# A graph-network layer: node stages in quads with transposes ahead, alphas and sums a step behind, target rows as three bf16 parts

## The chip, the cores and the metric

The kernel runs on one core of a Trainium2 chip. Its time is device microseconds, the median of several runs. Lines (L718) are those of the kernel before.

## What is computed

12,500 nodes with 128 channels, 400,000 edges sorted by target. All is fp32. In short:

```
h        = relu(layernorm(x))
message  = (h @ w_src + b_src)[src] + (h @ w_dst)[dst]
message *= edge_weight * (silu(silu(edge_attr @ w1 + b1) @ w2 + b2) @ w3 + b3)
sep      = message @ w_sep + b_sep           # per head (8): 16 for alpha, 16 for value
score    = sum_k smooth_leaky_relu(alpha)[k] * alpha_dot[k]
att      = softmax of score over the edges of one target
out      = x + segment_sum(value * att, dst) @ w_proj + b_proj
```

## The kernel before

**Node stage** (L140 to L290). x lies in SBUF as 98 tiles of 128 nodes, in groups of 14. For each group `stats` (layer-norm statistics on VectorE) and `norm` (ScalarE) of the next group are issued, then `products` of this one: for each quad of four tiles transposes on TensorE (L220), a VectorE copy `hT` (L223), products with both weight matrices (L230), and two copies out of PSUM, `ms`, one on ScalarE (L237) and one on VectorE that adds b_src (L238). The two tables of messages, `t_src` and `t_dst`, go to DRAM. After group 1, `ends_and_cuts` checks on VectorE that the edges are sorted and narrow enough for the fast path, and writes the first and last target of every section to DRAM.

**Setup of the windows** (L603 to L634): small loads of the doubled MLP weights, the windows' first targets (`tgt`) and `far`, all on SP's queue.

**The window loop** (`passes`, from L636; `step(k)`, k from -5 to 399). A step is 1000 edges in two sections of 500, each of four tiles of 125. A section's targets lie in a window of 64 nodes. The order of instructions on each engine is the order in which `step` issues them by hand:

- SP: the stores of step c-1, loads of edge weights, targets (`load_d`), the two windows' rows of `t_dst` (`load_md`), edge attributes (`load_e`, one of a step's eight tiles for eight steps at once) for later steps. c = k - 12 (`LAG`).
- `gather(k+4)`: eight indirect DMAs by GpSimd (L718) fetch the source rows into `gs`, of which there are four; each block waits for the last transposes of step k.
- `sums_begin(c)`: softmax weights copied into `pvx` (ScalarE), one-hot rows of targets `oh` (VectorE, L851).
- `mlp3(k)` (L758, then `rad` on VectorE, L761) and `message(k)`: eight transposes of gathered rows into PSUM (L770), onto which the target rows are accumulated as an fp32 one-hot product of 64 rows, one for each section (L775); `mT` = that times `rad` (L779).
- `values(c, 0)`, `alphas(k, 0)`, `values(c, 1)`: V = mT @ w_v of the step twelve back (L864), times weights into `pvx` (L866); pa = w_a @ mT (L783), its silu `sl` (L785) and `al` (L787).
- `mlp1(k+2)`, `mlp2(k+1)` (h on ScalarE, L739 and L746), `one_hot_T(k+1)` (`ohT`), `alphas(k, 1)`.
- `sums(c)`: 16 small products of `oh` and `pvx` (L875), copied out as `ob` (L879), stored in the next step.
- parts of the softmax of earlier steps, `e_T(k+3)` (transposes of edge attributes, L728), and in odd steps `scores(k)` of two steps (L794).

PSUM has eight banks: p3 two (shared by mlp1 and mlp3), m1 (mlp2 and e_T), pm two, pa, V, and `misc` (sums, scores, softmax and index transposes).

After the loop the last twelve steps are drained, partial sums of nodes that cross sections are combined and scattered into `agg` (L1067). **Final stage** (from L1130): groups of 14 tiles; GpSimd adds b_proj to x (L1162), VectorE divides by the weights' sums (L1165 to L1168), quads are transposed (L1179), copied (L1182), multiplied by w_proj (L1186), and x and a bias of the values are added on VectorE (L1185, L1190). A slower path for unsuitable inputs exists and isn't taken.

Of the kernel before, what the change touches and what calls it, by code (L numbers as in the profile page):

```python
# [21 lines left out]
F32 = mybir.dt.float32  # L22
# [30 lines left out]
LAG = 12  # L53
EP = 8
# [3 lines left out]
def gnn_kernel(ctx: ExitStack, tc: tile.TileContext, a: dict, out: bass.AP):  # L58
# [18 lines left out]
    agg = dram.tile([N + W, ROW], F32, name="agg")  # L77
    win = dram.tile([NS * W, ROW], F32, name="win")
    base_d = dram.tile([2, NP], I32, name="base_d")
# [15 lines left out]
    x_v = x[0:NF * P, :].rearrange("(p t) c -> p t c", t=NF)  # L95
    ident = const.tile([P, P], F32, name="ident")
# [48 lines left out]
    with tc.tile_pool(name="node", bufs=2) as np_, tc.tile_pool(name="node1", bufs=1) as n1, \  # L145
# [6 lines left out]
        b_nodes = n1.tile([P, C], F32, name="b_nodes")  # L152
        nc.scalar.dma_start(out=b_nodes, in_=a["b_src"].to_broadcast([P, C]))
# [6 lines left out]
        last = n1.tile([1, 2, NP], I32, name="last")  # L160
# [3 lines left out]
        nc.sync.dma_start(out=prev[1:RP, :], in_=dst[RC - 1:E - 1].rearrange("(p c) -> p c", c=RC))  # L164
        with nc.allow_non_contiguous_dma(reason="the sections' ends"):
            for f in range(2):
                nc.sync.dma_start(out=base[:, f, :], in_=dst_h[f:f + 1, :, 0])
                nc.sync.dma_start(out=last[:, f, :], in_=dst_h[f:f + 1, :, SEC - 1])
# [16 lines left out]
        spans = groups[:-1] + [(groups[-1][0], NB)]  # L185
        hs = {}

        def rows(t):
            return P if t < NF else tail

        def stats(g):
            t0, t1 = spans[g]
            for t in range(t0, t1):
                n = rows(t)
                st = np_.tile([P, nc.vector.BN_STATS_DIM], F32, name="st", bufs=4)
                nc.vector.bn_stats(st[:n], x_all[:n, t, :])
                nc.vector.bn_aggr(mv[:n, t, :], st[:n])
            s = slice(t0, t1)
            nc.scalar.activation(rstd[:, s], mv[:, s, 1], AF.Sqrt, bias=eps, scale=1.0)
            nc.vector.reciprocal(rstd[:, s], rstd[:, s])  # L200
            nc.vector.scalar_tensor_tensor(shift[:, s], mv[:, s, 0], -1.0, rstd[:, s],
                                           op0=ALU.mult, op1=ALU.mult)

        def norm(g):
            t0, t1 = spans[g]
            hs[g] = np_.tile([P, XG, C], F32, name="h")
            for t in range(t0, t1):
                n = rows(t)
                nc.scalar.activation(hs[g][:n, t - t0, :], x_all[:n, t, :], AF.Relu,
                                     bias=shift[:n, t:t + 1], scale=rstd[:n, t:t + 1])  # L210

        def products(g):
            t0, t1 = spans[g]
            ms = np_.tile([P, 2, XG, C], F32, name="ms")
            for u0 in range(t0, t1, 4):
                us = range(u0, min(u0 + 4, t1))
                pt = nps.tile([P, 4, P], F32, name="pt")
                for u in us:
                    n = rows(u)
                    nc.tensor.transpose(pt[:, u - u0, :n], hs[g][:n, u - t0, :], ident[:n, :n])  # L220
                hT = np_.tile([P, 4, P], F32, name="hT")
                w = (len(us) - 1) * P + rows(us[-1])
                nc.vector.tensor_copy(hT.rearrange("p u n -> p (u n)")[:, :w],  # L223
                                      pt.rearrange("p u n -> p (u n)")[:, :w])
                for v0 in range(0, len(us), 2):
                    vs = us[v0:v0 + 2]
                    pm = nps.tile([P, 2, 2, C], F32, name="pm", bufs=4)
                    for j, u in enumerate(vs):
                        n = rows(u)
                        nc.tensor.matmul(pm[:n, j], hT[:, u - u0, :n], w_nodes, start=True, stop=True)  # L230
                    i, m = vs[0] - t0, len(vs)
                    if rows(vs[-1]) == P:
                        cuts = [(P, 0, m)]
                    else:
                        cuts = [(P, 0, m - 1)] * (m > 1) + [(tail, m - 1, m)]
                    for n, j0, j1 in cuts:
                        nc.scalar.copy(ms[:n, 0, i + j0:i + j1, :], pm[:n, j0:j1, 0, :])  # L237
                        nc.vector.tensor_tensor(  # L238
                            ms[:n, 1, i + j0:i + j1, :], pm[:n, j0:j1, 1, :],
                            b_nodes[:n].unsqueeze(1).to_broadcast([n, j1 - j0, C]), op=ALU.add)  # L240
            f1 = min(t1, NF)
            for k, table in enumerate((t_src, t_dst)):
                tv = table[0:NF * P, :].rearrange("(p t) c -> p t c", t=NF)
                nc.sync.dma_start(out=tv[:, t0:f1, :], in_=ms[:, k, 0:f1 - t0, :])
# [4 lines left out]
        def ends_and_cuts():  # L249
# [5 lines left out]
            ends = n1.tile([1, 2 * NS + 2], I32, name="ends")  # L255
            nc.vector.memset(ends, -1)
            ev = ends[:, 1:2 * NS + 1].rearrange("o (k f c) -> o f k c", f=2, c=2)
            nc.vector.tensor_copy(ev[:, :, :, 0], base)
            nc.vector.tensor_copy(ev[:, :, :, 1], last)
            nc.sync.dma_start(out=base_d.rearrange("f k -> (f k)").unsqueeze(0),  # L260
                              in_=base.rearrange("o f k -> o (f k)"))
            nc.sync.dma_start(out=ends_d, in_=ends)
            nc.sync.dma_start(out=t_dst[N:N + W, :], in_=z[:W, 0:C])
            span = n1.tile([1, 2 * NP], F32, name="span")
            nc.vector.tensor_sub(span, last.rearrange("o f k -> o (f k)"),
                                 base.rearrange("o f k -> o (f k)"))
            nc.vector.tensor_scalar(span, span, float(W - 1), None, op0=ALU.is_ge)
            wide = n1.tile([1, 1], F32, name="wide")
            nc.vector.tensor_reduce(wide, span, AX.X, ALU.add)
            gt = n1.tile([RP, RC], BF16, name="gt")  # L270
            nc.vector.tensor_tensor(gt, prev, cur, op=ALU.is_gt)
            cnt = n1.tile([RP, 1], F32, name="cnt")
            nc.vector.tensor_reduce(cnt, gt, AX.X, ALU.add)
            tot = nps.tile([1, 1], F32, name="tot", bufs=1)
            nc.tensor.matmul(tot, cnt, ones[:RP, 0:1], start=True, stop=True)
            nc.vector.tensor_add(bad, tot, wide)

        G = len(spans)
        stats(0)
        norm(0)  # L280
        for g in range(G):
            if g + 1 < G:
                stats(g + 1)
                norm(g + 1)
            products(g)
            if g == 1:
                ends_and_cuts()
        w_score = const.tile([C, C], F32, name="w_score")
        nc.vector.tensor_scalar(w_score, heads, dot, 0.8, op0=ALU.mult, op1=ALU.mult)
# [313 lines left out]
    def windows():  # L603
        with tc.tile_pool(name="wk", bufs=1) as kp:
            w1b = kp.tile([P, P], F32, name="w1b")
            nc.vector.memset(w1b, 0.0)
            w2b = kp.tile([P, P], F32, name="w2b")
            nc.vector.memset(w2b, 0.0)
            w3b = kp.tile([P, C], F32, name="w3b")
            b12 = kp.tile([P, 2], F32, name="b12")  # L610
            for f in range(2):
                for q in range(2):
                    r = (2 * q + f) * RAD
                    nc.sync.dma_start(out=w1b[r:r + RAD, f * FC:(f + 1) * FC], in_=a["fc_w1"])
                s = slice(f * FC, (f + 1) * FC)
                nc.sync.dma_start(out=w2b[s, s], in_=a["fc_w2"])
                nc.sync.dma_start(out=w3b[s, :], in_=a["fc_w3"])
                nc.sync.dma_start(out=b12[s, 0:1], in_=a["fc_b1"])
                nc.sync.dma_start(out=b12[s, 1:2], in_=a["fc_b2"])
            w_s = kp.tile([C, 32], F32, name="w_s")  # L620
            nc.vector.memset(w_s, 0.0)
            nc.vector.tensor_copy(w_s[:, 0:H], w_score[:, 0:C:C // H])
            b_s = kp.tile([P, 1], F32, name="b_s")
            tgt = kp.tile([P, NP], F32, name="tgt")
            far = kp.tile([P, NS], BF16, name="far")
            with tc.tile_pool(name="tg", bufs=1) as gp, tc.tile_pool(name="tg_ps", bufs=1, space=PSUM) as gq:
                pb = gq.tile([P, 1], F32, name="pb")
                for j in range(4):
                    nc.tensor.matmul(pb[32 * j:32 * j + 32, :], w_s, b_a, start=True, stop=True)
                nc.vector.tensor_scalar(b_s, pb, 0.25, None, op0=ALU.mult)  # L630
                tb = gp.tile([P, NP], I32, name="tb")
                nc.sync.dma_start(out=tb[0:W, :], in_=base_d[0:1, :].to_broadcast([W, NP]))
# [605 lines left out]
```

## Time and profile before

| what | value |
|---|---|
| median of three runs | 6562.58 us (6560.19 to 6575.51) |
| profiled execution | 6566.2 us, its span 6564.2 us |
| granted TensorE clock, mean | 0.873 |
| busy PE / DVE / ACT / POOL | 77% / 44% / 27% / 47% |
| node stage | 0 to 194 us |
| setup, up to the first mlp3 | 194 to 239 us |
| 400 steps, first mlp3 to last | 239 to 6296 us |
| drain and combine | 6296 to 6410 us |
| final stage | 6410 to 6564 us |

PE is TensorE's matmuls, PEld its weight loads, DVE VectorE, ACT ScalarE, POOL GpSimd, SP the queue that issues most DMAs. A group's row gives line, engine, operation, output and input, count, then busy time, mean ns of one, and the engine's idle time just before it with what ended it. A timeline row gives start, duration, the instruction, and in brackets the idle time before it. An end of a matmul in the trace is modelled, so the time at which others get its result is seen in their starts.

### The profile page before, as it was taken

How to read it: one execution, taken by the hardware profiler on the slowest of the kernel's cores; microseconds unless marked ns; L12 is line 12 of the kernel's file. 1: busy time of each engine (PE TensorE's matmuls, PEld its weight loads, DVE VectorE, ACT ScalarE, POOL GpSimd, SP SyncE). 2: the span in 40 equal slices, each digit the busy share in tenths (PEclk: the TensorE clock that was granted, in tenths of full speed). 3: DMA queues.
4: the chain of work that ended last, by engine and by line, in shares of the span. 5: the costliest groups of instructions: out<-in, count | busy, mean ns of one | idle time of the engine just before them, and what ended most of it. 6: DMA issues, size and time to landing. Idle time of an engine off the chain costs nothing. (4 is left out here: it accounts for less than half of the span.)

```text
span 6564.2 us, 79188 instructions
## 1 busy us (share of the span) xinstructions
PE 5066.2 (77%) x26490; PEld 2665.6 (41%) x26490; DVE 2887.1 (44%) x5210; ACT 1785.1 (27%) x3797; POOL 3111.5 (47%) x3231
## 2 busy tenths in 40 slices
PE   3477878787878878788788787887887878888774
PEld 2234444444444444444444444444444444444453
DVE  4234444444444444444444444444444444444465
ACT  3122222222222222222222222222222222222221
POOL 0455555455554545544455454454554545545402
PEclk7688898898998989988888898898888989888885
DMA  3454444444444444444444444444444444444423
GB/s 124 135 144 119 124 119 115 125 117 121 121 122 118 121 119 119 124 117 115 123 120 121 119 116 121 122 115 120 121 117 122 119 120 121 124 119 118 114 60 123
DMA packets 884920, 783.25 MB, mean 119 GB/s; under 512 B 527255, under 2 KB 773279, under 8 KB 884250
## 3 DMA queue, kind: packets, MB, share of 16 engines
q1 hardware_dynamic: 778482, 560.72, 31.0%
q0 software_dynamic: 102816, 210.37, 13.6%
q10 hardware_dynamic: 3202, 6.99, 0.3%
q8 instruction: 212, 3.47, 0.2%
q14 instruction: 208, 1.70, 0.1%
HBM read 643.82 MB, written 134.27 MB: 119 GB/s over the span
## 5 line engine op out<-in xcount | busy, mean ns | idle before, releaser
L718 POOL DMA_INDIRECT gs<-t_src,idx x3200 | 3067.4, 959 | 3189.3 <-PE pm L770 1756.2
L787 DVE SCALAR_TENSOR_TENSOR al<-pa,sl 128x500 f32<-128x500 f32 x800 | 542.9, 679 | 1570.9 <-ACT sl L785 1022.1
L761 DVE SCALAR_TENSOR_TENSOR rad<-p,c_fc_b,w_b 128x500 f32<-128x500 f32 x800 | 553.6, 734 | 1389.4 <-PE p L758 1102.0
L783 PE MATMUL pa<-mT,c_w_a 128*128 128x500 f32 x1600 | 833.7, 603 | 256.8 <-DVE mT L779 248.1
L785 ACT ACTIVATE sl<-pa,c_b_a 128x500 f32<-128x500 f32 x800 | 541.4, 677 | 1789.4 <-PE pa L783 626.9
L864 PEld LDWEIGHTS V<-c_w_v,mT 128*125 128x125 f32 x6208 | 741.2, 188 | 634.8 <-issue 337.9
L864 PE MATMUL V<-c_w_v,mT 128*125 128x128 f32 x6208 | 891.3, 286 | 23.2 <-issue 1.1
L794 PE MATMUL misc<-al,w_s 128*32 128x500 f32 x1600 | 365.9, 986 | 539.5 <-ACT ob L879 525.3
L779 DVE TENSOR_TENSOR mT<-pm,rad 128x500 f32<-128x500 f32 x800 | 504.3, 672 | 280.1 <-PE pm L775 252.8
L758 PE MATMUL p<-h,w3b 64*128 64x500 f32 x1600 | 625.5, 870 | 0.0
L770 PEld LDWEIGHTS pm<-ident,gs 125*128 125x128 f32 x3200 | 430.1, 169 | 435.9 <-issue 435.9
L866 DVE TENSOR_TENSOR pvx<-V,Pem 125x512 f32<-125x512 f32 x776 | 528.9, 682 | 44.4 <-PE m L744 26.5
L770 PE MATMUL pm<-ident,gs 125*128 125x125 f32 x3200 | 533.6, 321 | 0.0
L875 PEld LDWEIGHTS misc<-pvx,oh 125*64 125x64 f32 x6400 | 365.5, 137 | 322.4 <-issue 279.7
L875 PE MATMUL misc<-pvx,oh 125*64 125x136 f32 x6400 | 473.0, 287 | 28.2 <-DVE pvx L866 27.6
L783 PEld LDWEIGHTS pa<-mT,c_w_a 128*128 128x128 f32 x1600 | 269.5, 191 | 500.6 <-DVE mT L779 287.4
L775 PE MATMUL pm<-ohT,md 64*128 64x500 f32 x1600 | 471.0, 656 | 0.1
L739 ACT ACTIVATE h<-p,b 128x500 f32<-128x500 f32 x400 | 270.5, 676 | 700.9 <-PE pa L783 157.2
L879 ACT COPY ob<-misc 128x136 f32<-128x136 f32 x400 | 108.7, 272 | 1292.5 <-remote 630.5
L744 PE MATMUL m<-h,w2b 128*128 128x500 f32 x800 | 449.6, 644 | 0.0
L728 PE MATMUL m<-ident,e_t 125*128 125x125 f32 x800 | 187.4, 319 | 204.4 <-ACT h L746 169.8
L746 ACT ACTIVATE h<-m,b 128x500 f32<-128x500 f32 x400 | 270.7, 677 | 223.4 <-PE m L744 55.0
(145 smaller groups left out, 3153.1 us busy)
## 6 DMA issues: line engine op xcount, KB each, us to landing
w_b<-in_edge_weight SPq DMA_DIRECT2D x400, 500.0 KB
d_b<-in_dst SPq DMA_DIRECT2D x400, 250.0 KB
gs<-t_src,idx POOLq DMA_INDIRECT x3200
e_t<-in_edge_attr SPq DMA_DIRECT2D x400, 125.0 KB
sc_d<-Sp SPq DMA_DIRECT2D x200, 250.0 KB
win<-ob SPq DMA_DIRECT2D x400, 68.0 KB
agg<-ob SPq DMA_DIRECT2D x800, 33.5 KB
md<-t_dst SPq DMA_DIRECT2D x800, 32.0 KB
```

Source lines behind the costliest of these rows:

```text
L718: nc.gpsimd.indirect_dma_start(out=gs[:, j, :], out_offset=None, in_=t_src[:, :], in_offset=bass.IndirectOffsetOnAxis(ap=idx[:, t:t + 1], ...
L758: nc.tensor.matmul(p3[:, f, 0:SEC], w3b[s, :], h2s[k][s, :], start=True, stop=True)
L761: nc.vector.scalar_tensor_tensor(rads[f], p3[:, f, 0:SEC], b3, w_g[k][:, f * SEC:(f + 1) * SEC], op0=ALU.add, op1=ALU.mult)
L770: nc.tensor.matmul(pm[f][:, t * T:(t + 1) * T], gs[:T, f * TS + t, :], ident[:T, :T], start=(t == 0), stop=False, is_transpose=True, skip_ ...
L775: nc.tensor.matmul(pm[f], md[k][s, :], ohT[k][s, :], start=False, stop=True, skip_group_check=True)
L779: nc.vector.tensor_mul(mTs[k][:, f * SEC:(f + 1) * SEC], pm[f], rads[f])
L783: nc.tensor.matmul(pa, w_a, mTs[k][:, f * SEC:(f + 1) * SEC], start=True, stop=True)
L785: nc.scalar.activation(sl, pa, AF.Silu, bias=b_a, scale=1.0)
L787: nc.vector.scalar_tensor_tensor(al, pa, 0.25, sl, op0=ALU.mult, op1=ALU.add)
L864: nc.tensor.matmul(V[:, t, :], mTs[c][:, o:o + T], w_v, start=True, stop=True)
L866: nc.vector.tensor_mul(pvx[c][:, f, :, 0:C].rearrange("p t (h k) -> p t h k", h=H), V.rearrange("p t (h k) -> p t h k", h=H), Pem[c // MP] ...
L875: nc.tensor.matmul(acc[f * W:(f + 1) * W, :], ohs[c][:, f * TS + t, :], pvx[c][:, f, t, :], start=(t == 0), stop=(t == TS - 1), skip_group ...
```

## The change

- **Order of the loop.** `alphas` run for step k-1 instead of k, `sums` for c-1 with c = k-13, `scores(k-1)` at the end of even steps; stores are those of c-2. V(c, 0) goes ahead of `message`, V(c, 1) behind `mlp1`. The second half of `sums_begin`, `one_hot(c)`, goes behind the second alphas. Softmax parts come a step later.
- **Target rows.** `split_md` writes the 64-row windows of `t_dst` as three bf16 parts whose sum is the fp32 value (two ScalarE copies, two VectorE subtractions), and `ohT` is bf16. The one-hot product becomes six bf16 products in place of two in fp32.
- b_src is added where `mT` is made (`b_n`), no longer in the node stage. One `e_t` load per step in the edges' own order; mlp1's activation and `rad` reorder accordingly. `rad` is one buffer.
- **x + b_proj** is made during the loop (`load_x`, `add_x`, every eighth step from 45 on) in a DRAM tensor `xb`; the final stage loads that.
- **Node stage** in quads: statistics eight tiles ahead, `norm` two quads ahead, transposes (`turn`) one quad ahead; `ms` copied mostly by ScalarE. The check is split (`fits` after quad 12, `cuts` at the end), the windows' setup goes into this stage, `base_d` is dropped.
- **Final stage** in groups of twelve tiles, transposes one quad ahead, result written over x and stored by quads.

The core of the diff, the loop first:

```diff
-LAG = 12
-EP = 8
+LAG = 13
...
+            def split_md(k, i):
+
+                if i == 0:
+                    m3[k] = lp.tile([P, 3, C], BF16, name="m3")
+                    nc.scalar.copy(m3[k][:, 0, :], md[k])
+                elif i == 1:
+                    mr[k] = lp.tile([P, C], F32, name="mr")
+                    nc.vector.tensor_sub(mr[k], md.pop(k), m3[k][:, 0, :])
+                elif i == 2:
+                    nc.scalar.copy(m3[k][:, 1, :], mr[k])
+                else:
+                    nc.vector.tensor_sub(m3[k][:, 2, :], mr.pop(k), m3[k][:, 1, :])
...
-                for f in range(2):
-                    s = slice(f * W, (f + 1) * W)
-                    nc.tensor.matmul(pm[f], md[k][s, :], ohT[k][s, :], start=False, stop=True,
-                                     skip_group_check=True)
+                for j in range(3):
+                    for f in range(2):
+                        s = slice(f * W, (f + 1) * W)
+                        nc.tensor.matmul(pm[f], m3[k][s, j, :], ohT[k][s, :], start=False, stop=(j == 2),
+                                         skip_group_check=True)
                 mTs[k] = sp.tile([C, PR], F32, name="mT", bufs=LAG + 1)
                 for f in range(2):
-                    nc.vector.tensor_mul(mTs[k][:, f * SEC:(f + 1) * SEC], pm[f], rads[f])
+                    s = slice(f * SEC, (f + 1) * SEC)
+                    nc.vector.scalar_tensor_tensor(mTs[k][:, s], pm[f], b_n, rad[:, s], op0=ALU.add, op1=ALU.mult)
...
+            def add_x(i):
+                t = xs.pop(i)
+                for n, t0, t1 in blocks(*quads[i]):
+                    u = t[:n, t0 - quads[i][0]:t1 - quads[i][0], :]
+                    nc.vector.tensor_tensor(u, u, b_out[:n].unsqueeze(1).to_broadcast([n, t1 - t0, C]), op=ALU.add)
+                    nc.sync.dma_start(out=xb_v[:, t0:t1, :] if n == P else xb[NF * P:N, :].unsqueeze(1), in_=u)
...
                 if has(k + 4):
                     gather(k + 4)
+
                 if has(c):
-                    sums_begin(c)
-                if has(k):
-                    message(k, mlp3(k))
+                    weights(c)
+                rad = mlp3(k) if has(k) else None
                 if has(c):
                     values(c, 0)
                 if has(k):
-                    alphas(k, 0)
-                if has(c):
-                    values(c, 1)
+                    message(k, rad)
+                if has(k + 1):
+                    split_md(k + 1, 0)
+                if has(k - 1):
+                    alphas(k - 1, 0)
+                if has(k + 1):
+                    split_md(k + 1, 1)
+                if has(c - 1):
+                    sums(c - 1)
                 if has(k + 2):
                     mlp1(k + 2)
                 if has(k + 1):
+                    split_md(k + 1, 2)
+                if has(c):
+                    values(c, 1)
+                if has(k + 1):
+                    split_md(k + 1, 3)
                     mlp2(k + 1)
                     one_hot_T(k + 1)
-                if has(k):
-                    alphas(k, 1)
-                if has(c):
-                    sums(c)
+                if has(k - 1):
+                    alphas(k - 1, 1)
...
+                if has(c):
+                    one_hot(c)
                 if has(k + 3):
                     e_T(k + 3)
-                if has(k) and k % 2 == 1:
-                    scores(k)
+                if has(k - 1) and k % 2 == 0:
+                    scores(k - 1)
...
+        stats(0, 4)
         norm(0)
-        for g in range(G):
-            if g + 1 < G:
-                stats(g + 1)
-                norm(g + 1)
-            products(g)
-            if g == 1:
-                ends_and_cuts()
+        stats(4, G)
+        norm(1)
+        turn(0)
+        for i in range(Q):
+            if i % 2 == 0 and 4 * i + G < NB:
+                stats(4 * i + G, min(4 * i + 2 * G, NB))
+            if i + 2 < Q:
+                norm(i + 2)
+            if i + 1 < Q:
+                turn(i + 1)
+            products(i)
+            if i == 12:
+                fits()
+        cuts()
...
+        quotients(0)
+        turn(0)
+        for i in range(Q):
+            if i % 3 == 0 and i // 3 + 3 < NG:
+                load_g(i // 3 + 3)
+            if i % 3 == 1 and i // 3 + 1 < NG:
+                quotients(i // 3 + 1)
+            if i + 1 < Q:
+                turn(i + 1)
             finish(i)
```

## Prediction

> **What bounds the kernel now.** I read the page's table of costly groups first, then busy time by stage, then the timeline of one pair of steps. No engine is full: over the span PE is busy 77%, POOL 47%, DVE 44%, ACT 27%. The groups tell what waits:
>
> ```profile
> L718 POOL DMA_INDIRECT gs<-t_src,idx x3200 | 3067.4, 959 | 3189.3 <-PE pm L770 1756.2
> L794 PE MATMUL misc<-al,w_s 128*32 128x500 f32 x1600 | 365.9, 986 | 539.5 <-ACT ob L879 525.3
> L879 ACT COPY ob<-misc 128x136 f32<-128x136 f32 x400 | 108.7, 272 | 1292.5 <-remote 630.5
> ```
>
> Half of POOL's time passes before gathers, mostly for the transposes that free their buffer. PE waits 525 us in front of the scores for the copy of the sums, and that copy waits for nothing that the trace can name ("remote"). By stage (columns: length, then busy time of PE, PEld, DVE, ACT, POOL, granted clock, DMA):
>
> ```profile
> 0.00:194.00 194.00, 83.69 (x296) 62.87 (x296) 91.40 (x305) 58.93 (x156) 1.59 (x9) 0.79 0.31 115
> 194.00:239.00 45.00, 7.97 (x28) 3.62 (x30) 3.81 (x17) 3.96 (x6) 17.65 (x19) 0.50 0.55 144
> 239.00:6296.00 6057.00, 4833.45 (x25386) 2486.15 (x25386) 2630.90 (x4633) 1687.74 (x3550) 3049.74 (x3182) 0.89 0.46 120
> 6410.00:6564.00 154.00, 71.32 (x296) 58.54 (x296) 90.72 (x161) 16.14 (x29) 34.52 (x13) 0.53 0.34 129
> ```
>
> The window loop is 92% of the span: 6057/399 = 15.18 us a step. By the starts of mlp3, steps alternate: about 12.2 us from even to odd, 18.2 from odd to even. The timeline of one pair shows why:
>
> ```profile
> 3016.51 1.15 PE L875 MATMUL misc<-pvx,oh 125*64 125x136 f32 x16
> ...
> 3018.96 0.94 POOL L718 DMA_INDIRECT gs<-t_src,idx  x1 [0.30 <-issue]
> ...
> 3021.63 0.27 ACT L879 COPY ob<-misc 128x136 f32<-128x136 f32 x1 [4.34 <-PE pm L775]
> ...
> 3028.51 1.15 PE L875 MATMUL misc<-pvx,oh 125*64 125x136 f32 x16
> ...
> 3030.98 0.94 POOL L718 DMA_INDIRECT gs<-t_src,idx  x1 [0.30 <-issue]
> 3033.76 0.27 ACT L879 COPY ob<-misc 128x136 f32<-128x136 f32 x1 [2.32 <-remote]
> ...
> 3034.08 1.90 PE L794 MATMUL misc<-al,w_s 128*32 128x500 f32 x8 [3.57 <-ACT ob L879]
> ...
> 3037.52 2.04 PE L758 MATMUL p<-h,w3b 64*128 64x500 f32 x4
> ...
> 3041.34 0.94 POOL L718 DMA_INDIRECT gs<-t_src,idx  x1 [9.42 <-PE pm L770]
> ```
>
> The sums end at 3017.66, their copy starts at 3021.63, though ACT was free. The last gather of that block ended at 3019.90, 1.73 us before. In the next step again: sums end 3029.66, last gather 3031.92, copy 3033.76. I lined up all steps by their gather block: whatever PE finishes inside a block reaches its waiters late, in a burst some 1.8 us after the last gather ends; ACT's and DVE's signals do not. Eight gathers start 1.25 us apart, a block is 9.68 us. So a period cannot be below about 9.68 + 1.8 + 0.5 (transposes signalled, next gather issued) = 12.0. Even steps already run at that. Odd steps add scores, which share the sums' bank: PE sits idle 3.57 us, the clock then falls to 0.5 for 6.83 us (3033.74 to 3040.57), scores take 1.90 instead of 1.0 and mlp3 2.04 instead of 1.03, and only then come the transposes that POOL waits for (9.42 us).
>
> **The change, part by part.**
> *Loop, PE's order.* Sums of c-1 and alphas of k-1 are issued from tiles a step old, and scores follow at the end of even steps, after mlp2 and e_T. The sums' signal still comes at the flush after the block, but scores now come after it: the 3.57 us wait goes, and with no gap of that size the clock should stay at 1. The odd step then loses 3.57 + 0.9 + 1.0 and the slower transposes (1.58 instead of 1.07), 6.0 us in all, which is exactly 18.2 - 12.2. What is late next is the gather round trip, 12.0 us. PE's own work must fit beneath: mlp3 1.03, two V 2.14, transposes 1.07, one-hot product, pa 1.7, sums 1.15, mlp1 0.62, mlp2 1.04, e_T 0.43, half a scores 0.53: 9.7 plus the product, 10.4 us. It fits.
> *One-hot product.* Four fp32 instructions (two passes for each of two sections, in different row halves, starting together) take 1.11 us. Six bf16 ones replace them: as three overlapping pairs near 0.65, one after another up to 1.3. I take 0.7, since the fp32 pairs overlap. PE is covered by the round trip: worth 0 either way; without that cover -0.4 to +0.2 us a step (-155 to +77).
> *Split.* A step gains two ACT copies and two DVE subtractions of 128x128, nearest rows 0.27 (ob) each: 0.54 on ACT (27% busy) and 0.54 on DVE (44%). They wait for the row loads issued three steps ahead. Each later part waits for the other engine; behind ACT's second copy stands h2, which releases m1 and mlp3; behind DVE's subtractions pvx and ohT. Taken at 0 because both engines have 6 us of idle a step; 0.54 x 386 = 208 if not. The Trainium skill speaks against these subtractions: SBUF — State Buffer, "Who interferes with whom", says that a VectorE instruction with two SBUF inputs contends with a GpSimd one that reads SBUF, one blocking the other whole. By the rule the gathers would lose up to those 0.54 us, 208 in the loop. The trace disagrees: the oh comparison (0.67 us, two SBUF inputs) starts at 3017.92 inside the gather of 3017.72, and the next gather comes at 3018.96, the usual 1.24 later. I take 0.
> *b_n, rad, h1 layout.* Same instruction counts; mT becomes a three-operand form as rad (0.73 against 0.67): 0.12 a step on DVE, covered. One rad buffer makes mlp3's readers wait for the last mT, which ended long before: 0.
> *Queues.* One e load a step in place of one of eight tiles every step keeps SP's issues; the stores of c-2 move SP past nothing that waits. load_x and add_x: 25 times a load, an addition of 128x512 (0.6 by L1190) and a store, 15 us of DVE in 3200, at 0; POOL's queue has only gathers, as before.
> *LAG 13:* one more step to drain, the first twelve steps differ little. They have no V and sums, and ran 15.5 us each; I leave 13 of them so.
> *Node stage.* Per group PE waited 72.2 us for hT, DVE 84.6 for ACT's copy. With transposes one quad ahead the quad costs its busiest engine: PE 4 x 0.325 + 8 x 0.35 = 4.1 at half clock, less at full; DVE 4 x 0.444 + 0.61 = 2.4; ACT 4 x 0.4 + 2 x 0.48 = 2.6. At 3.5 x 25 = 88, from 16 (first rows of x landed) to 104; the blocks of the sorted check still cost DVE 18, half of it covered. The setup of 45 us moves beneath it: e loads that were 15.3 us of SP issue go to two DMAs, and the first gather to mlp3 remains 22.7. First mlp3 at about 140 instead of 238.6: -99. Bounds -50 (SP's dozen small loads and the gates of the tables stay) and -115.
> *Final stage.* POOL's bias addition (29.7 us, while the multiply-add beside it takes 4 us and more) goes:
>
> ```profile
> L1185 DVE SCALAR_TENSOR_TENSOR x_fin<-v_out,has,x_fin 128x128 f32<-128x128 f32 x98 | 49.4, 562 | 0.0
> L1162 POOL TENSOR_TENSOR x_fin<-x_fin,c_b_out 128x1792 f32<-128x1792 f32 (+2 forms) x8 | 29.7, 3742 | 9.4 <-DVE r L1165 9.3
> ```
>
> 98 multiply-adds at 0.28 make 27, so 22 saved; transposes ahead take most of PE's 40.6 us waits for q. I take 154 to 103; bounds 94 and 144 (loads of agg still first, clock 0.53).
>
> **The sum,** in the profiled execution's time (span 6564.2, execution 6566.2, the median of the runs 3.6 below). A loop step: 12.0, plus hiccups where pa's signal of an even step misses its place and waits for the flush (2.3 to 5 us in some steps; ten in a hundred give 0.4): 12.4. First mlp3 140; first 13 steps 13 x 15.5 = 201; 386 x 12.4 = 4786; drain and combine 114 as before; final 103; 2 around the span: 5346. Less 3.6: 5340.
>
> **The rivals.**
> A, above: the step at the gather round trip. 0.55. Range 5200 to 5500.
> B, partial: in even steps scores need the second al, which needs sl and so pa, whose signal falls in the gather block; released only at its end, the even step takes 17.1, the odd 12.0, mean 14.55. 386 x 14.55 = 5616; total 6176 less 4: about 6170. For it: pa's signals were up to 4.4 us late in one of ten even steps. Against: pa now follows from a tile a step old and is issued early in the step. 0.23, 5550 to 6500.
> C, better: signals are held less in the new order, and the step falls to PE's 10.4 or POOL's 10.0 a step: about 10.3, total 4536. Against: the lateness was there in every order of PE's work I could find, bursts of the first steps included. 0.09.
> D, slower: mlp2 follows split and V, so its matmul slips. In before it is issued 5.5 us after the block's start and mostly gets through; past about 7 it would be held to the flush like the sums. Then h2, e_T (same bank) and mlp3 follow the flush, and the next transposes behind them: 15.9 and 16.9, mean 16.4, loop 6330, total 6890. It turns slower where the mean step passes (6566 - 360 - 201)/386 = 15.56. For it: ACT's second part waits for DVE, and h2 stands behind. Against: V and sums need nothing of the step itself, so mlp2 comes at about 5.1. 0.13. That the change does nothing is covered by the ends of B and D; mT and split alone cannot, by their sizes.
>
> **How the numbers follow.** Likeliest A: 5340. The range must leave no more than 0.2 out: from 5000 (between A and C) to 6300 (most of B); D and the fast half of C lie outside, about 0.18. A's own range stands above. Faster by over 0.3% (what a measurement of this kernel can tell from no change): A, B, C, 0.87; D nearly all slower, 0.12; same 0.01.
>
> **What would show it.** Loop: steps even in length near 12.2, gathers' idle near 2.3 us a block, no idle of PE before scores, granted clock near 1 in the loop. One-hot product row: six per step starting in pairs 0.2 apart. B: two lengths again, even the longer, with al waiting for sl. D: h2 waiting long for mlp2 in each step. Node: first mlp3 near 140; final stage near 103 with multiply-adds at 0.28. The prediction is wrong above all if the late signals are not tied to the gathers.

## The result, and the profile after

The changed kernel took 7244.2 us (median of four runs, 7228.0 to 7255.5) beside 6568.8 for the kernel before: ratio 1.103 (1.100 to 1.106), slower by a tenth. The forecast was 5340. It lies near the prediction's rival D (6890), the held mlp2, to which it had given 0.13. At some times the kernel before took 4921 to 4927 us instead of 6536 to 6629 (one chip showed both), and PE's signals were then not late, so each number below stands beside that of before taken with it.

By stage, the changed kernel (same columns as before; loop from the first mlp3 to the last):

```profile
0.00:168.00 168.00, 79.86 (x326) 55.04 (x326) 77.32 (x289) 69.92 (x165) 8.93 (x17) 0.80 0.48 160
168.00:7029.00 6861.00, 4981.79 (x26133) 2630.57 (x26132) 2915.14 (x5451) 1833.08 (x4340) 3016.50 (x3193) 0.83 0.43 108
7029.00:7137.00 108.00, 69.01 (x541) 55.36 (x541) 72.19 (x99) 20.72 (x63) 1.48 (x3) 0.86 0.20 52
7137.00:7237.00 100.00, 42.42 (x295) 40.05 (x295) 67.25 (x169) 15.83 (x27) 11.34 (x12) 0.77 0.55 202
```

The front lost 71 us and what comes after the last mlp3 60 (208 instead of 268). The loop alone gained 804: 6861/399 = 17.2 us a step instead of 15.18, and both lengths are now long (17.7 and 17.0 in the mean). PE's busy time grew at a lower clock, 0.83 instead of 0.89.

The groups tell where the wait went. First three of the kernel before (reader of V, reader of mlp2, e_T), then those of the changed kernel:

```profile
L866 DVE TENSOR_TENSOR pvx<-V,Pem 125x512 f32<-125x512 f32 x776 | 528.9, 682 | 44.4 <-PE m L744 26.5 <-PE p L736 9.9 <-issue 5.5
L746 ACT ACTIVATE h<-m,b 128x500 f32<-128x500 f32 x400 | 270.7, 677 | 223.4 <-PE m L744 55.0 <-PE pa L783 53.5 <-issue 52.5
L728 PE MATMUL m<-ident,e_t 125*128 125x125 f32 x800 | 187.4, 319 | 204.4 <-ACT h L746 169.8 <-DMA e_t<-in_edge_attr 14.0 <-ACT h L739 11.0
...
L739 POOL DMA_INDIRECT gs<-t_src,idx x3200 | 3023.8, 945 | 3967.9 <-PE pm L796 2923.3
L896 DVE TENSOR_TENSOR pvx<-V,Pem 125x512 f32<-125x512 f32 x774 | 532.9, 689 | 2211.5 <-remote 1593.8
L749 PE MATMUL m<-ident,e_t 125*128 125x125 f32 x800 | 230.6, 383 | 1693.8 <-ACT h L769 1526.0
L822 PE MATMUL misc<-al,w_s 128*32 128x500 f32 x1600 | 527.9, 835 | 112.0 <-ACT Pem L868 54.7
L769 ACT ACTIVATE h<-m,b 128x500 f32<-128x500 f32 x400 | 270.8, 677 | 1252.2 <-remote 908.2
```

PE's 539.5 us in front of the scores, 525 of them for the copy of the sums, are down to 112.0, as forecast. In their place PE waits 1694 us in front of e_T (L749; 204 before), for ACT's reader of mlp2 (L769, which gives the m1 bank free), and that one waits for "remote", a signal that the profile ties to no instruction, as the copy of the sums did in the kernel before. VectorE's pvx waits likewise, 1594 us. Then the transposes come late and POOL's idle time grows by 779. One step of the timeline (start, duration, instruction, idle before it):

```profile
3773.14 0.94 POOL L739 DMA_INDIRECT gs<-t_src,idx  x1 [5.45 <-PE pm L796]
...
3774.57 1.15 PE L905 MATMUL misc<-pvx,oh 125*64 125x136 f32 x16
...
3776.27 1.14 PE L894 MATMUL V<-c_w_v,mT 128*125 128x128 f32 x8
...
3777.24 1.00 PE L767 MATMUL m<-h,w2b 128*128 128x500 f32 x2
...
3781.88 0.94 POOL L739 DMA_INDIRECT gs<-t_src,idx  x1 [0.30 <-issue]
3783.01 0.69 DVE L896 TENSOR_TENSOR pvx<-V,Pem 125x512 f32<-125x512 f32 x1 [6.69 <-remote]
...
3783.72 0.68 ACT L769 ACTIVATE h<-m,b 128x500 f32<-128x500 f32 x1 [4.13 <-remote]
...
3784.45 0.68 PE L749 MATMUL m<-ident,e_t 125*128 125x125 f32 x2 [5.37 <-ACT h L769]
...
3785.06 2.04 PE L781 MATMUL p<-h,w3b 64*128 64x500 f32 x4
...
3789.77 0.94 POOL L739 DMA_INDIRECT gs<-t_src,idx  x1 [6.95 <-PE pm L796]
```

The sums now stand 1.4 us into the gather block. V ends at 3777.41 and mlp2 at 3778.24; both readers start more than 5 us later, just after the block's last gather has ended (3782.82). PE has nothing to do for 5.37 us, its granted clock is 0.5 from 3781.21 to 3788.04 (mlp3 2.04 us), and the next gather starts 16.6 us after the first of this block.

### The profile page after: what moved, and what is told of

Read it like the earlier page. It is cut to its first block, busy times and chain, and to the rows that moved or that the text cites. A ratio compares the mean times of both kernels' runs of the same rounds, so it can differ in the third digit from the quotient of the medians.

```text
span 7237.2 us, 84066 instructions
## 1 busy us (share of the span) xinstructions
PE 5173.1 (71%) x27292; PEld 2781.0 (38%) x27292; DVE 3131.9 (43%) x6006; ACT 1939.5 (27%) x4595; POOL 3038.2 (42%) x3223
## 4 chain that ended last, share of the span: by engine, by line
PE 68%; another core or an unknown queue 14%; ACT 7%; issue 5%; DVE 3%; SPq 1%; DMA 1%; POOL 0%; ACTq 0%; POOLq 0%; DVEq 0%
PE V L894 14%; PE pa L811 11%; PE p L781 9%; PE misc L822 6%; PE misc L905 6%; PE pm L796 6%; PE m L767 5%; PE pm L802 4%; PE p L758 4%; PE m L749 3%; ACT h L769 3%; ACT h L761 2%; ACT sl L813 1%; ACT m L730 1%
## 5 line engine op out<-in xcount | busy, mean ns | idle before, releaser
L739 POOL DMA_INDIRECT gs<-t_src,idx x3200 | 3023.8, 945 | 3967.9 <-PE pm L796 2923.3
L749 PE MATMUL m<-ident,e_t 125*128 125x125 f32 x800 | 230.6, 383 | 1693.8 <-ACT h L769 1526.0
L894 PEld LDWEIGHTS V<-c_w_v,mT 128*125 128x125 f32 x6192 | 916.3, 227 | 622.9 <-issue 310.2
L894 PE MATMUL V<-c_w_v,mT 128*125 128x128 f32 x6192 | 1081.8, 328 | 0.0
L749 PEld LDWEIGHTS m<-ident,e_t 125*128 125x128 f32 x800 | 101.7, 178 | 1988.8 <-ACT h L769 1765.3
L781 PE MATMUL p<-h,w3b 64*128 64x500 f32 x1600 | 728.4, 1005 | 0.0
L807 DVE SCALAR_TENSOR_TENSOR mT<-pm,c_b_n,rad 128x500 f32<-128x500 f32 x800 | 553.7, 734 | 389.7 <-PE pm L802 320.9
L822 PE MATMUL misc<-al,w_s 128*32 128x500 f32 x1600 | 527.9, 835 | 112.0 <-ACT Pem L868 54.7
L769 ACT ACTIVATE h<-m,b 128x500 f32<-128x500 f32 x400 | 270.8, 677 | 1252.2 <-remote 908.2
L796 PE MATMUL pm<-ident,gs 125*128 125x125 f32 x3200 | 487.3, 304 | 0.0
L767 PE MATMUL m<-h,w2b 128*128 128x500 f32 x800 | 405.7, 589 | 0.0
L781 PEld LDWEIGHTS p<-h,w3b 64*128 64x128 f32 x1600 | 188.7, 289 | 358.1 <-issue 175.0
```

The lines of the kernel that those rows point to most:

```text
L739: nc.gpsimd.indirect_dma_start(out=gs[:, j, :], out_offset=None, in_=t_src[:, :], in_offset=bass.IndirectOffsetOnAxis(ap=idx[:, t:t + 1], ...
L749: nc.tensor.transpose(pe[:, g, :], ev[:, g, :], ident[:T, :T])
L767: nc.tensor.matmul(p2, w2b, h1s.pop(k), start=True, stop=True)
L781: nc.tensor.matmul(p3[:, f, 0:SEC], w3b[s, :], h2s[k][s, :], start=True, stop=True)
L796: nc.tensor.matmul(pm[f][:, t * T:(t + 1) * T], gs[:T, f * TS + t, :], ident[:T, :T], start=(t == 0), stop=False, is_transpose=True, skip_ ...
L807: nc.vector.scalar_tensor_tensor(mTs[k][:, s], pm[f], b_n, rad[:, s], op0=ALU.add, op1=ALU.mult)
```

## The experiments

Late means here: from the modelled end of PE's result to the start of its reader, while the reader's engine was free. "In the middle" is the median over the loop's steps. All edits are to the changed kernel; every time but e5's is of a single run. The diffs are cut to the lines that move, in their new order; a line without a sign only shows the place.

### Are the gathers what holds the signals?

**e1 and e9: no gathers after the first four steps.**

```diff
                 if has(k + 4):
-                    gather(k + 4)
+                    if k < 0:
+                        gather(k + 4)
+                    else:
+                        gath[k + 4] = gath[k]
```

> The changed kernel, but the source rows are gathered for the first four steps only and those buffers are read again in all later steps, so the result lacks the right source rows. Theory H (PE's signals are held back while gathers are under way, and mlp2's is the one that hurts): the waits of pvx and h2 for signals long due vanish and the step falls from 17.2 to PE's own 10.4 to 11.5 us, total 4750 to 5200. Rival S (the split of the target rows and its ACT/DVE chain, or the new order as such, sets the step): no gather is in that chain, total stays above 6500.

> As e1: the changed kernel with source rows gathered for the first four steps only. If before takes about 6560 here: theory G (the gathers under way hold PE's signals back) expects no late pvx and h2 and 4700 to 4900, as in e1; theory X (a state of the chip in which PE's signals are slow by themselves) expects above 6500. If before takes about 4930 it tells nothing new: 4743.

e1: 4743 us beside 4927, and as nothing was late in before then, it tells little by itself. e9: 4756 beside 6629. The row of pvx in e9:

```profile
L896 DVE TENSOR_TENSOR pvx<-V,Pem 125x512 f32<-125x512 f32 x774 | 530.8, 686 | 388.6 <-PE V L894 388.2
```

No "remote" is left; pvx waits for V itself. The kernel without gathers is as fast where before takes 6629 as where it takes 4927. So the lateness needs the gathers (theory G); PE is not slow by itself. What of the gathers it needs is not told: with GpSimd's instructions go their data and nearly all signals of the transposes that the gathers wait for (PE gives 5417 signals instead of 8544).

**e5 and e16: the changed kernel again.**

> The changed kernel, unaltered, on the chip of an experiments' call. The kernel before took 4927 us in the last call and 6569 us in the comparison, so the time of one and the same kernel differs by a third between calls. If the held signals belong to the gathers themselves (theory H), they show again here and the time is near 7244 beside 6569. If they belong to a chip or to what else runs on it, and not to the kernel (theory X), then where the kernel before takes about 4927 this one takes 4750 to 4850, as the three variants of the last call (4776 to 4828) did; and where before takes about 6570 it takes about 7244.

> The changed kernel, unaltered. If before takes about 6560 here: 7200 to 7280 as in the comparison and in e5. If before takes about 4930, this one takes 4750 to 4850, since there e2 to e4 stand at 4776 to 4828.

e5: 7257 us beside 6558, ratio 1.108 (1.099 to 1.117), the same as the comparison. e16: 4753 beside 4924, which is 3.5% faster. Its loop and two of its rows:

```profile
168.00:4550.00 4382.00, 4218.10 (x26185) 2285.95 (x26182) 2900.53 (x5458) 1838.44 (x4344) 3142.89 (x3193) 0.99 0.69 170
```

```profile
L769 ACT ACTIVATE h<-m,b 128x500 f32<-128x500 f32 x400 | 270.8, 677 | 368.9 <-PE m L767 359.6 <-PE V L894 9.3
L749 PE MATMUL m<-ident,e_t 125*128 125x125 f32 x800 | 172.4, 297 | 3.9 <-ACT h L769 3.5 <-DMA e_t<-in_edge_attr 0.4
```

With signals on time PE is busy 96% of the loop at a clock of 0.99, the step is 10.96 us, and e_T waits 4 us in all instead of 1694. The gathers then cost next to nothing: e1, without them, took 4743. The same instructions kept PE busy 4982 us in the late case: 764 us more, at the lower clock. Why one and the same kernel has late signals at one time and not at another stays open.

### Is it the split, or the order?

**e2 and e10: the fp32 one-hot product back, no split.**

```diff
-                ohT[k] = sp.tile([P, SEC], BF16, name="ohT")
+                ohT[k] = sp.tile([P, SEC], F32, name="ohT")
...
-                        nc.tensor.matmul(pm[f], m3[k][s, j, :], ohT[k][s, :], start=False, stop=(j == 2),
...
+                    nc.tensor.matmul(pm[f], md[k][s, :], ohT[k][s, :], start=False, stop=True,
...
-                    split_md(k + 1, 0)
...
```

> The changed kernel with the fp32 one-hot product back (two fp32 products, no split). Theory H: the split stands behind the late signals and does not make them late; 7244 moves by less than 1.5% (7140 to 7350). Rival S: the split's two ACT copies and two DVE subtractions delay h2 and pvx; without them about 1 to 2 us a step come back, 6450 to 6850.

> As e2: the changed kernel with the fp32 one-hot product and no split. If before takes about 6560 here: theory O expects 7000 to 7350 (the split is not what makes mlp2's signal late); rival S, that the split's ACT and DVE instructions cost the time, expects 6450 to 6700. If before takes about 4930: 4828.

e10: 7255 beside 6629, against 7244 beside 6569 and 7257 beside 6558 with the split: no difference beyond the 1% that before itself moved. Rival S, which expected 6450 to 6700, falls. e2 met signals on time (4828 beside 4927), so it does not decide; against e16 it says that the bf16 parts are then worth 4828 - 4753 = 75 us, 0.19 a step.

**e3 and e6: the order of before inside the step, all else kept.**

```diff
-                rad = mlp3(k) if has(k) else None
-                if has(c):
-                    values(c, 0)
-                    message(k, rad)
-                    alphas(k - 1, 0)
-                    sums(c - 1)
...
+                    one_hot(c)
+                    message(k, mlp3(k))
+                    values(c, 0)
+                    alphas(k, 0)
+                    values(c, 1)
                     mlp1(k + 2)
-                    values(c, 1)
                     mlp2(k + 1)
-                    alphas(k - 1, 1)
+                    alphas(k, 1)
+                    sums(c)
...
-                    scores(k - 1)
+                    scores(k)
```

> The changed kernel with the order of before inside the step (alphas of k, sums of c behind the second alphas, scores at odd steps, one-hot ahead of mlp3), the split and everything else of the change kept. Theory H: the order alone decides; the steps are again near 12.2 and 18.2, and with the shorter node and final stages the total is 6380 to 6550. Rival S: stays above 6900.

> The changed kernel with the order of before inside the step, as in e3, to be read beside the kernel before in the same call. If before takes about 6560 here: theory O (the order decides which of PE's late signals somebody waits for) expects steps of 12.2 and 18.2 again and 6380 to 6550 in all; the rival S (the split's work) 6900 or more. If before takes about 4930: 4776 as in e3.

e6: 6523 beside 6623; steps 12.7 and 18.1, near those of the kernel before. The order alone makes the 7244: 721 us between e6 and the changed kernel. In e3 signals were on time (4776 beside 4927); the new order is then worth 22 us (4753 in e16).

### Which move of the order?

**e11: the sums at the very end of the step. e12: the second V behind mlp2, the sums left ahead.**

```diff
# e11
-                if has(c - 1):
-                    sums(c - 1)
                 if has(k + 2):
                     mlp1(k + 2)
...
                     scores(k - 1)
+                if has(c - 1):
+                    sums(c - 1)
# e12
-                if has(c):
-                    values(c, 1)
...
                     one_hot_T(k + 1)
+                if has(c):
+                    values(c, 1)
```

> The changed kernel with one move undone in part: sums(c-1) stand at the end of the step, behind the scores, instead of ahead of mlp1. If before takes about 6560 here: if the sums, coming 2.5 us into a gather block, are what puts mlp1's, V's and mlp2's signals into the row of late ones (theory M), mlp2 is then about as late as in the kernel before (under 1 us in the middle) and the total is 5500 to 6500. If the second V ahead of mlp2 does it (theory V), mlp2 stays 2 us or more late in the middle and the total above 6800. If before takes about 4930: 4700 to 4850.

> The changed kernel with the second V issued behind mlp2 instead of ahead of it, sums left where the change put them. If before takes about 6560 here: theory V (V ahead of mlp2, whose reader pvx and whose signal come first) expects mlp2 less than 1 us late in the middle and 5500 to 6500 in all. Theory M (the sums ahead) expects mlp2 still 1.5 us or more late and the total above 6700. If before takes about 4930: 4700 to 4850.

e11: 6320 beside 6543, within what theory M expected. e12: 7017 beside 6543. Rows of e11, then of e12:

```profile
L896 DVE TENSOR_TENSOR pvx<-V,Pem 125x512 f32<-125x512 f32 x774 | 531.1, 686 | 133.2 <-PE V L894 42.2 <-PE m L767 27.5 <-issue 22.5
L769 ACT ACTIVATE h<-m,b 128x500 f32<-128x500 f32 x400 | 270.1, 675 | 300.9 <-issue 110.9 <-PE pa L811 80.8 <-remote 57.3
L825 ACT ACTIVATE Sp<-misc,b_s 128x500 f32<-128x500 f32 x200 | 135.4, 677 | 597.9 <-remote 457.1 <-PE misc L822 108.3 <-issue 32.3
```

```profile
L896 DVE TENSOR_TENSOR pvx<-V,Pem 125x512 f32<-125x512 f32 x774 | 532.5, 688 | 1111.2 <-remote 570.1 <-PE m L749 202.9 <-PE p L781 150.3
L769 ACT ACTIVATE h<-m,b 128x500 f32<-128x500 f32 x400 | 271.8, 680 | 145.8 <-remote 58.9 <-PE pa L811 35.4 <-issue 20.6
```

In e11 "remote" is gone from pvx and nearly from mlp2's reader; what is late now is the scores (457 us), which stand in front of the sums' bank. In e12 mlp2 is in time and V behind it is not. The middle lateness of each result inside a block, with the time of its end after the block's start:

| result | before | changed | e11, sums last | e12, V behind |
|---|---|---|---|---|
| mlp1 | 4.5 us: 0.1 | 3.2: 1.2 | 2.1: 0 | 3.2: 1.2 |
| second V | 3.9: 0 | 4.3: 4.9 | 3.2: 0 | 5.1: 2.7 |
| mlp2 | 5.5: 0.1 | 5.1: 3.4 | 4.0: 0 | 4.2: 0 |
| second pa | 6.3: 0.1 | 6.0: 0 (its reader stands behind mlp2's) | 4.9: 0.1 | 6.0: 2.9 |
| sums | 7.4: 3.7 | 2.6: 0.9 | 9.4: 1.6 | 2.6: 0.9 |

With the sums ahead, of the results that end between 3 and 6 us one or the other is late by several us; with the sums last all of them come in time in the middle. e12 went halfway: mlp2's reader was under 1 us late, as theory V said, but the time stayed above 6700, as theory M said, as V and pa took its place. So it is the sums' place that costs the most, not V's. It is not the whole of it: in e6, with the sums behind, mlp1 (ending at 4.6) is still 1.2 us late in the middle.

The table shows readers, and a reader's engine can be busy while the signal is still missing. The trace also records when the signals themselves counted, and this shows more. All of PE's signals raise one and the same semaphore, a counter (8544 times in the changed kernel); here they are paired with PE's results in order. In the step shown above the sums, mlp1, V, mlp2 and pa ended at 3775.72, 3776.34, 3777.41, 3778.25 and 3779.09. Their updates came at 3777.26, 3778.70, 3782.99, 3783.70 and 3784.44, each 0.02 to 0.08 us before the reader's start, which bears the pairing out: 1.5, 2.4, 5.6, 5.5 and 5.4 us late. On one counter a result cannot be announced before those ahead of it. In 268 of the changed kernel's 392 gather blocks every result has its update in the record; in 253 of them the sums' signal is the first that is over 0.3 us late. The late row begins with the sums, and V, mlp2 and the second pa stand in it (4.3, 5.5 and 5.4 us late in the middle; the 0 of pa in the table is only its reader waiting behind mlp2's). In e12 mlp2's own signal was 1.4 us late. In e16 none of 8372 paired signals came over 0.1 us late, in e9 none of 5410. What holds the first of a row back is not shown: in e6 and e8 mlp1 or V can be the first.

### Do orders that respect it reach 12 us?

**e4 and e7: mlp2 right behind message, V of the first section behind it, e_T and mlp1 ahead of the sums, second V behind them.**

```diff
                     message(k, mlp3(k))
+                    mlp2(k + 1)
+                    values(c, 0)
                     alphas(k - 1, 0)
+                    e_T(k + 3)
                     mlp1(k + 2)
+                    sums(c - 1)
+                    values(c, 1)
```

> The changed kernel with mlp2 right behind message (the first thing PE finishes in a gather block), V of the first section behind it, e_T and mlp1 ahead of the sums, the second V behind the sums, scores last. Theory H: mlp2's signal goes through, the transposes of the next step come on time, and the step falls to 12.0 to 13.5 us: total 5150 to 5800. Rival S: the number of instructions on ACT and DVE is the same, so above 6900.

> The changed kernel with mlp2 right behind message and V of the second section behind the sums, as in e4. If before takes about 6560 here: theory O expects that h2 comes on time and the step is 12 to 14 us, 5150 to 6000 in all; if PE's signals are late wherever they stand in the order (theory L: the lateness grows with PE's work in a gather block), no order helps and the time stays above 6500. If before takes about 4930: 4789 as in e4.

e4 met signals on time (4789 beside 4927) and does not decide. e7: 6660 beside 6623. mlp2's reader is in time there (0.04 us in the middle), but the sums are 5.0 us late and V behind them 4.3, and PE waits 458 us for the copy of the sums before the scores:

```profile
L822 PE MATMUL misc<-al,w_s 128*32 128x500 f32 x1600 | 541.5, 885 | 605.4 <-ACT ob L909 458.1 <-DVE al L815 60.7 <-issue 47.7
```

Theory O gave 5150 to 6000: a miss.

**e8: e6 with the scores of a pair one step later, behind the transposes of the even step.**

```diff
                     message(k, mlp3(k))
+                if has(k - 1) and k % 2 == 0:
+                    scores(k - 1)
...
-                if has(k) and k % 2 == 1:
-                    scores(k)
```

> e6 (the changed kernel with the step order of before) with one more edit: the scores of a pair are issued one step later, behind the transposes of the even step, so that PE does not stand in front of them for the copy of the held sums; softmax parts one step later. If before takes about 6560 here: theory O (what matters is who waits for a late signal; only the scores wait for the sums) expects the 18 us steps to fall to 12 to 13.5 and the total to 5200 to 5800. Theory L (late signals find another waiter in any order) expects 6300 or more. If before takes about 4930: 4700 to 4850.

e8: 6322 beside 6629, 4.6% faster, but far from 5200 to 5800. In steps that have scores ahead, mlp1 is 4.0 us late in the middle, in the others 1.1:

```profile
3762.89 0.68 ACT L761 ACTIVATE h<-p,b 128x500 f32<-128x500 f32 x1 [6.55 <-remote]
...
3765.07 0.68 PE L749 MATMUL m<-ident,e_t 125*128 125x125 f32 x2 [4.65 <-ACT h L769]
```

The late signal found another waiter, as theory L has it (above 6300).

**e15 and e18: mlp1 and mlp2 ahead of both V, scores of two steps back in odd steps behind message, sums at the end.**

```diff
                     message(k, mlp3(k))
+                    scores(k - 2)
                     alphas(k - 1, 0)
                     mlp1(k + 2)
                     mlp2(k + 1)
+                    values(c, 0)
                     alphas(k - 1, 1)
                     values(c, 1)
                     e_T(k + 3)
+                    sums(c - 1)
```

> The changed kernel in an order meant for late signals: mlp3, message, scores of the pair two steps back (odd steps), first alphas, mlp1, mlp2, then V of both sections, second alphas, e_T, and the sums at the very end, so that everything that the next step's first work needs is signalled ahead of the sums and nobody waits for their copy within a block. If before takes about 6560 here: theory M expects steps of 12 to 13.5 and 5200 to 5800 in all. If late signals find another waiter in any order (theory L): above 6200. If before takes about 4930: 4700 to 4850.

> As e15: the order with mlp1 and mlp2 ahead of V and the sums at the very end. If before takes about 6560 here: theory M expects steps of 12 to 13.5 and 5200 to 5800 in all; theory L (late signals find another waiter in any order) above 6200. If before takes about 4930: 4620 as in e15.

4620 beside 4924 and 4601 beside 4921: where signals are on time it is faster than the kernel before by 6.2% and 6.5%, and than the changed one (4753). No run of it met late signals, so whether it holds up there is not shown.

### What of the sums does it?

**e13 and e17: two of the sums' eight products. e14: the eight over all 128 columns.**

```diff
# e13
-                for t in range(TS):
-                    for f in range(2):
-                        nc.tensor.matmul(acc[f * W:(f + 1) * W, :], ohs[c][:, f * TS + t, :],
...
+                for f in range(2):
+                    nc.tensor.matmul(acc[f * W:(f + 1) * W, :], ohs[c][:, f * TS, :],
...
# e14
-                        nc.tensor.matmul(acc[f * W:(f + 1) * W, :], ohs[c][:, f * TS + t, :],
...
+                        nc.tensor.matmul(acc, ohs[c][:, 2 * t:2 * t + 2, :].rearrange("p a b -> p (a b)"),
...
```

> The changed kernel with only the first two of the sums' eight products (a quarter of their instructions; three quarters of each section's edges are left out of the result). If before takes about 6560 here: if the late signals begin with the sums' short products (theory M), V and mlp2 behind them are late by under 1 us in the middle (before: 3.4 for mlp2 in the changed kernel) and the total is 5300 to 6300. If any PE work ahead of them does it, or the mere place in the gather block (theory P), the total stays above 6800. If before takes about 4930: 4550 to 4750.

> As e13: the changed kernel with a quarter of the sums' products (three quarters of the edges left out). If before takes about 6560 here: theory M (the sums' short products start the lateness) expects mlp2 under 1 us late in the middle and 5300 to 6300 in all; theory P (the place in the block, or any PE work) 6800 or more. If before takes about 4930: 4547 as in e13.

> The changed kernel with the eight products of the sums each over all 128 columns, one after another, instead of pairs in the two column halves (the result's rows are mixed, the number of instructions is the same, PE takes about 1.8 us for them instead of 1.1). If before takes about 6560 here: if the column halves are what makes the signals late (theory C), mlp2 is in time and the total falls to 5500 to 6500 in spite of the longer products. If their number or the mere PE work counts, 7200 or more. If before takes about 4930: 5000 to 5200.

4547, 4580 and 5055, all beside 4924: no signal was late in these runs, so they do not tell. Against e16 they price PE's time: three quarters of the sums are worth 174 to 207 us over 400 steps, 0.4 to 0.5 a step, and giving up the column halves costs 302, 0.75 a step.

## Why the prediction was wrong, point by point

- **What bounds the kernel.** Right in the main: late signals of PE, and the scores behind the sums' copy. With gathers gone the lateness is gone (e9). Too strong was "whatever PE finishes inside a block reaches its waiters late": in the kernel before the second V, mlp1, mlp2 and the second pa end inside the block and are at most 0.1 us late in the middle; only the sums (3.7) and what stands behind them are held.
- **The step that failed** is in case A: "the 3.57 us wait goes", and "What is late next is the gather round trip, 12.0 us." The wait did go (539.5 to 112.0 us), but the sums, moved ahead, held mlp2 with them: its reader 3.4 us late in the middle, 1694 us of PE's wait before e_T. The step became 17.24 us where 12.4 was summed; over 386 steps that is 1868 of the 1893 us between the sum's 5346 and the 7239 of the profiled execution.
- **Why it seemed safe:** against D the text set "V and sums need nothing of the step itself, so mlp2 comes at about 5.1", and the point of decision "past about 7". mlp2 did come at 5.1. It was late all the same, since lateness is not set by the place in the block alone: the sums ahead of a result count (e11), as all share one counter. The prediction had taken a result's lateness from where it stood in the old order, and moved the sums without moving that. D was right about who waits for the held mlp2; its condition was wrong, and its size low: 17.24 measured against 16.4 is 324 us.
- **C** (PE-bound, 10.3 a step, 4536) is what happens where signals are on time: 10.96 and 4753 (e16).
- **One-hot product, split:** taken at 0, and no difference clear of noise in e10, though PE was covered by late signals and not by a 12.0 us round trip. The six bf16 products took 0.81 us a step (326.1 busy over 400), not 0.7.
- **Gathers beside VectorE:** taken at 0; with signals on time the mean gather is 985 ns with the split (e16) and 971 without (e2), 0.1 us a step, against the 0.54 feared. The Trainium skill, SBUF — State Buffer, "Who interferes with whom", which the prediction sets against the split, also says that `tensor_tensor` was not seen to stall DMA; these means agree with that.
- **Node stage:** 140 forecast, 168 measured. Longer by 28, within its bounds: the last products ended at 144.7 where 104 was forecast. ACT's copies waited 35.9 us for stores of t_dst, and PE 61.8 for ACT's norm, so PE did not set the quad as forecast; that ACT did is argued from these waits, not tested.
- **Final stage:** 103 forecast, 100; drain 114, 108. The multiply-adds fell from 562 ns to 345, not to 280:

```profile
L1259 DVE SCALAR_TENSOR_TENSOR x_fin<-v_out,has,x_fin 128x128 f32<-128x128 f32 x98 | 27.8, 345 | 0.0
```

- **Chances.** D deserved more: the prediction said of every result inside a block that it comes late, and then took mlp2 out of that by its place alone.

## What to carry over

Where a result's signal comes long after its producer's end, moving its consumer out of the way is half a remedy: ask which results then stand behind it, and who waits for those. Moving what comes late to the end helped here: the sums moved last brought 7244 to 6320. Moving what is needed early to the front, with the sums still ahead of others, did less (e7, 6660), and both at once (e15) was not seen with late signals. The sign of a change may hang on such waits: here 10% slower with late signals, 3.5% faster without.

## What the hardware showed

PE's signals reached ACT and VectorE late while GpSimd's gathers were under way; in the changed kernel one in ten readers of V started 7.3 us or more after V's end. In the timelines shown the kernel before got its held ones 1.7 us after the last gather's end (3021.63 against 3019.90), the changed kernel 0.2 us after it (3783.01 against 3782.82). The Trainium skill, TensorE: Matmul & The Clock Gate, "The cost: per-tile semaphore tail", prices the signals of packed matmuls at 26.3 ns each, one after another; a dozen of them would make an estimated 0.3 us by that rule. Once released, 13 held signals of the kernel before did come within 0.46 us (3021.61 to 3022.07), so the 3.4 us measured for mlp2 is something else. Products that fill only part of the columns (sums 64, scores 32) stood ahead of the latest results in the changed kernel and in e8; that they are the cause was argued and not shown, as e13, e14 and e17 ran where nothing was late. Open too are what of the gathers holds a signal, and why the lateness comes and goes. Where signals are late the trace also holds fewer of ACT's (2905 of 4126 in the changed kernel, 4051 of 4126 in e16); whether the two belong together is not shown.
